# Two bottleneck blocks on one core: the mixed stage's centring in 20 small VectorE operations, its transfers on one queue, and the border's sums and first rows on GpSimd

## The chip, the cores and the metric

The kernel runs on one core of a Trainium2 chip. A core has five engines that run their own instruction streams and wait for each other through semaphores: TensorE (PE in the profile; its weight loads are PEld), VectorE (DVE), ScalarE (ACT), GpSimd (POOL) and SyncE (SP), which here does nothing but issue transfers (DMAs). ACT and GpSimd can issue transfers too. The metric is the device time of one execution in microseconds (us). Before the change it is 1934.73 us, the median of 3 runs (1934.0 to 1935.46).

## The reference

Two residual bottleneck blocks, one after the other, on 64 images of 14 x 14 with 1024 channels, all in float32. The second block has weights of its own. Every batch norm takes its mean and variance from the batch.

```python
def _bn(x, gamma, beta):
    mean = jnp.mean(x, axis=(0, 2, 3), keepdims=True)
    var = jnp.var(x, axis=(0, 2, 3), keepdims=True)
    xn = (x - mean) * jax.lax.rsqrt(var + EPS)
    return gamma.reshape(1, -1, 1, 1) * xn + beta.reshape(1, -1, 1, 1)

def _L0_conv_ref(x, w1, b1, g1, be1, w2, b2, g2, be2, w3, b3, g3, be3, residual_scale):
    out = jax.nn.relu(_bn(_conv(x, w1, b1, 1, 0), g1, be1))     # 1x1, 1024 -> 256
    out = jax.nn.relu(_bn(_conv(out, w2, b2, 1, 1), g2, be2))   # 3x3, 256 -> 256
    out = _bn(_conv(out, w3, b3, 1, 0), g3, be3)                # 1x1, 256 -> 1024
    out = jax.nn.softplus(residual_scale)[0] * out
    out = x + out
    return jax.nn.relu(out)
```

## The kernel before

**Tiles.** The 64 images are 32 tiles of two images, 392 pixels each. Channels lie on the 128 partitions: 1024 channels are 8 slots (`CS`), 256 are 2 slots (`MS`). The output of a block's 3x3 convolution, `y_all`, stays on the chip as a whole: per partition 2 slots of 32 x 392 pixels.

**Stages, by the trace.** The first 1x1 convolution of block 0 runs to about 300 us, its 3x3 convolution to 586, then the *mixed stage* (`mixed`, L1434 to L1650) to about 820, a short *border* to 844, and then `fused`, in which the third convolution of block 0 and the first of block 1 alternate, to about 1280. Block 1's 3x3 convolution and its final stage take the rest.

**Why there is a mixed stage.** The batch norm behind the third convolution needs the mean and variance of the convolution's output. For tiles 16 to 31 (`KEPT` = 16) the stage computes that output, takes its statistics and stores it in DRAM (`z`). For tiles 0 to 15 it computes only the Gram matrix of the convolution's input, from which the statistics follow, and the convolution itself is done later, in `fused`. TensorE alternates between the two.

**The convolution part.** `first()` does tile 16 plainly, with eight outputs, and prepares tile 17 behind the first of them. Then `direct_stream` (L597) runs 60 *units*, four for each of the tiles 17 to 31 (unit = 4 x (tile - 17) + q). A unit is a `Direct`: a 2 x 2 block product done with 7 products of half-size blocks, for which sums of the input's blocks (`ct`, four for each tile) and of the weights are needed. Each unit takes 7 steps, each with one product of this unit or of the one before it: p1 of this unit, p7 of the one before, p5, p2 and p6 of this one, p4 and p3 of the one before. The products land in PSUM banks (`cy`, `cp`, `cx`, `ay`). ACT copies them out (into `kept`, or into the buffers `cu` and `cx`), and DVE adds (L584 and L590) and takes statistics (L595). A bank is free for a later product only when its reader on ACT or DVE is done. `kept` has four slots, one for each q. After a unit's last add its slot goes out to `z` in one transfer on SP's queue (L592; `put`, L1536, for tile 16), and the unit four later writes the same slot again, at its step 2, which has to wait until the transfer has landed.

**The input of a unit.** `prepare(t)` works a tile ahead, on GpSimd: for each of the two slots two operations (`normed_less`, L1510) that scale, shift, clip at 0 and subtract a constant `c` (add `minus_c`), and then four sums of 128 x 196 (`column_sums`, L470 to L473). The loop takes its three steps in units with q = 0 and 1.

**The Gram part.** Tiles 0 to 15 are 6272 pixels, cut into five pieces (`MOVES`: four of 1280 and one of 1152). Each piece goes through this chain:

- *norm* (`norm_piece`): ACT, in 8 parts, one per unit at step 1 (the first 8 in `first()`);
- *centring* (`center`, L1450): `minus_c` is added, one operation for each of the two slots;
- *move* (`move`, L1481): 16 transfers bring `y_all` to `home` with the 32-pixel blocks so arranged that a 32 x 32 transpose on DVE gives pixels on partitions. There are two `home` buffers. Move 0 comes after `first()`, the moves 1 to 4 at the units 9, 17, 25 and 33;
- *transposes* (`turn`, L1244): DVE, 512 columns each, into `zt`;
- *Gram products* (`gram_products`, L159 with `ap<-zt`): TensorE, 32 products at step 2 of the units 9, 12, 15 and so on up to 45. `batches` hands them out: products at step 2, then the transposes of the next batch at step 3 of this unit and of the next.

At units 20, 23, 26 and 29 DVE also combines weights of the next block at step 3 (`summed_a`).

**Order.** Everything in this stage is held in program order on each engine: the order in which the code issues it. So an operation that waits holds up all that stands behind it on its engine, and a transfer on SP's queue stands behind the ones issued before it. `pinned` extends this to helpers that use `run`.

**The border.** When the statistics are there, `residual` finishes tile 0, and `fused` starts: the third convolution of the first kept tiles (`Conv3`, whose block sums are made in `column_sums`, here on DVE), rows of tiles that come back from `z` (`kept_rows`: for odd o GpSimd scales L1798 and adds L1799, for even o DVE does both in one operation L1801), and the first convolution of block 1 (`Conv1`, with copies `au` on ACT). GpSimd also adds for `Conv3` (L530, L535). ACT's relus of finished rows and its copies stand in one order.

**The constant.** `minus_c` is computed once for each block, at the block's start (L2058), into one buffer of a pool under one name: the second block's write has to wait for the last reader of the first block's.

## Time and profile before

| | |
|---|---|
| median of 3 runs | 1934.73 us (1934.0 to 1935.46) |
| the profiled execution | 1934.27 us |
| its span in the trace | 1932.5 us |
| mean granted TensorE clock | 0.994 |
| instructions | 28607 |

The span goes from the first to the last instruction that the profiler recorded; the execution's own time is 1.8 us longer. The timeline view has one row for each instruction, or run of like instructions: start in us, length in us, engine, line of the kernel, operation, output <- input by the program's names, shape, count, and in brackets the idle time of the engine just before it with what ended that. "SPq" is SP's queue of transfers. Matmuls all have L159, and ACT's operations L332, since helpers issue them: they are told apart by what they write and read. The windows view gives the busy time of each engine in a stretch, with the number of instructions in brackets, then the granted TensorE clock (1.00 is full speed), the share of time in which the transfer engines were busy, and the GB/s moved.

### The profile page before, as it was taken

How to read it: one execution, taken by the hardware profiler on the slowest of the kernel's cores; microseconds unless marked ns; L12 is line 12 of the kernel's file. 1: busy time of each engine (PE TensorE's matmuls, PEld its weight loads, DVE VectorE, ACT ScalarE, POOL GpSimd, SP SyncE). 2: the span in 40 equal slices, each digit the busy share in tenths (PEclk: the TensorE clock that was granted, in tenths of full speed). 3: DMA queues.
4: the chain of work that ended last, by engine and by line, in shares of the span. 5: the costliest groups of instructions: out<-in, count | busy, mean ns of one | idle time of the engine just before them, and what ended most of it. 6: DMA issues, size and time to landing. Idle time of an engine off the chain costs nothing. (4 is left out here: it accounts for less than half of the span.)

```text
span 1932.5 us, 28607 instructions
## 1 busy us (share of the span) xinstructions
PE 1890.3 (98%) x9778; PEld 1567.6 (81%) x9778; DVE 1578.1 (82%) x2454; ACT 1089.1 (56%) x2275; POOL 768.1 (40%) x772
## 2 busy tenths in 40 slices
PE   9999999999998889989999999999999999999999
PEld 5555557999996778889999999989999987555555
DVE  5777768999996666777888878789999987888886
ACT  2222214677775454455555555546777782666666
POOL 0111100211206646166777677602112041766665
PEclk9999999999999999999999999999999999999999
DMA  7777634887953445677877789748878557699997
GB/s 290 276 246 267 221 148 158 206 222 201 228 188 121 137 147 167 203 280 279 312 269 287 289 311 263 265 148 208 222 214 216 166 148 278 249 334 342 342 356 280
DMA packets 261986, 458.20 MB, mean 237 GB/s; under 512 B 59152, under 2 KB 228464, under 8 KB 248656
## 3 DMA queue, kind: packets, MB, share of 16 engines
q1 hardware_dynamic: 224608, 374.23, 57.8%
q0 software_dynamic: 31472, 29.47, 7.7%
q10 hardware_dynamic: 5760, 52.67, 6.8%
q8 instruction: 78, 1.28, 0.3%
q14 instruction: 68, 0.56, 0.1%
HBM read 289.44 MB, written 141.03 MB: 223 GB/s over the span
## 5 line engine op out<-in xcount | busy, mean ns | idle before, releaser
L332 ACT ACTIVATE x<-x,shift 128x392 f32<-128x392 f32 x452 | 260.0, 613 | 80.5 <-DVE x L507 31.4
L159 PE MATMUL columns<-v,ub 128*128 128x224 f32 (+1 forms) x1536 | 302.4, 338 | 1.1 <-ACT columns L332 0.8
L159 PEld LDWEIGHTS columns<-v,ub 128*128 128x128 f32 x1536 | 268.8, 188 | 7.0 <-ACT columns L332 1.5
L332 ACT ACTIVATE cu<-cy,scale 128x196 f32<-128x196 f32 (+1 forms) x360 | 175.7, 500 | 167.0 <-PE cy L159 159.9
L159 PE MATMUL ay<-at,ws 128*128 128x196 f32 (+1 forms) x768 | 194.1, 384 | 5.1 <-ACT au L332 3.8
L159 PEld LDWEIGHTS ay<-at,ws 128*128 128x128 f32 x768 | 137.3, 191 | 40.5 <-ACT au L332 4.1
L507 DVE SCALAR_TENSOR_TENSOR x<-cp,scale,x 128x196 f32<-128x196 f32 (+1 forms) x240 | 124.5, 519 | 46.2 <-PE cp L159 44.8
L634 POOL TENSOR_TENSOR x<-x,cu 128x392 f32<-128x392 f32 x120 | 125.8, 1049 | 73.0 <-DVE x L507 71.8
L332 ACT ACTIVATE au<-ay 128x196 f32<-128x196 f32 (+1 forms) x140 | 53.9, 385 | 173.9 <-PE ay L159 159.7
L159 PE MATMUL l<-diffs,ub 128*128 128x224 f32 (+1 forms) x768 | 149.6, 337 | 0.3 <-ACT sd L1894 0.3
L159 PE MATMUL m<-sums,ua 128*128 128x224 f32 (+1 forms) x752 | 146.0, 336 | 0.2 <-DVE sums L750 0.2
L159 PEld LDWEIGHTS l<-diffs,ub 128*128 128x128 f32 x768 | 134.6, 189 | 1.2 <-ACT sd L1894 0.6
L159 PEld LDWEIGHTS m<-sums,ua 128*128 128x128 f32 x752 | 131.5, 189 | 1.3 <-DVE sums L750 0.7
L159 PE MATMUL cx<-y,w 128*128 128x196 f32 (+1 forms) x396 | 126.2, 404 | 0.8 <-ACT cx L332 0.8
L1048 POOL DMA_DIRECT2D y<-f x24 | 32.7, 1683 | 231.8 <-DVE f L968 231.8
L530 POOL TENSOR_TENSOR x<-x,cu 128x196 f32<-128x196 f32 (+1 forms) x120 | 104.5, 871 | 50.9 <-ACT cu L332 22.5
L159 PE MATMUL cy<-y,w 128*128 128x196 f32 (+1 forms) x364 | 115.4, 404 | 1.8 <-POOL y L1510 1.0
L535 POOL TENSOR_TENSOR x<-x,cu 128x392 f32<-128x392 f32 x60 | 79.2, 1320 | 86.1 <-DVE x L507 83.2
L332 ACT ACTIVATE y<-y,shift,scale 128x1568 f32<-128x1568 f32 (+7 forms) x94 | 106.7, 1154 | 6.6 <-DVE shift L1926 6.5
L206 POOL DMA_DIRECT2D u<-y x48 | 26.0, 545 | 212.0 <-ACT y L332 211.3
L159 PE MATMUL cy<-ct,wt 128*128 128x196 f32 x400 | 100.3, 333 | 5.8 <-ACT cu L332 4.7
L1798 POOL TENSOR_SCALAR y<-y,scale 128x392 f32<-128x392 f32 x57 | 94.0, 1649 | 29.4 <-DVE scale L2116 29.4
(298 smaller groups left out, 4551.6 us busy)
## 6 DMA issues: line engine op xcount, KB each, us to landing
ub<-u SPq DMA_DIRECT2D x92, 768.0 KB, 5.2
x<-in_x SPq DMA_DIRECT2D x35, 1568.0 KB, 8.2
mid<-x ACTq DMA_DIRECT2D x32, 1568.0 KB, 8.4
x<-mid SPq DMA_DIRECT2D x32, 1568.0 KB, 8.9
out<-x SPq DMA_DIRECT2D x123, 392.0 KB, 8.1
x<-in_x SPq DMA_DIRECT2D x108, 392.0 KB, 8.1
z<-kept SPq DMA_DIRECT2D x64, 392.0 KB, 3.0
ua<-u SPq DMA_DIRECT2D x92, 256.0 KB, 3.0
```

Of the source, the lines that this page charges most:

```text
L159: tc.keep_in_program_order(nc.tensor.matmul(*args, **kw))
L206: nc.gpsimd.dma_start(out=us[b][i][:, s, o], in_=u)
L332: tc.keep_in_program_order(nc.scalar.activation(*args, **kw))
L507: run(nc.vector.scalar_tensor_tensor(v, bank, self.scale[:, o : o + 1], v, ALU.mult, ALU.add))
L530: run(nc.gpsimd.tensor_add(self.part(1, 1), self.part(1, 1), u3))
L535: run(nc.gpsimd.tensor_add(v, v, self.u12))
L634: nc.gpsimd.tensor_add(v, v, self.u12[:, i * self.n : (i + 1) * self.n])
L1048: nc.gpsimd.dma_start(out=out_rows[3][:, o], in_=fa[:, o, :full], accum_op=ALU.add)
L1798: run(nc.gpsimd.tensor_scalar(z, z, scale[:, o : o + 1], None, ALU.mult))
```

## The change

1. *Centring.* Each piece is centred in four operations (two halves of 640 columns, or 576, for each of the two slots) in place of two, and all of them are on VectorE; before, GpSimd did one slot of the pieces 1 to 4. The loop issues one half at step 3 of a unit as soon as the norm parts that it needs have been issued, as long as a move is still to come: by the order of the instructions that is every even unit from 2 to 32. The four halves of piece 0 come one after another behind `first()`.
2. *Move 0.* All 16 transfers are on SP's queue; before, every second one was on GpSimd's.
3. *Preparation.* The generators of `prepare` are made ahead (`coming`), and `first()` also takes the two `normed_less` steps of tile 18. The loop goes on from there: sums of tile 18, `normed_less` of tile 19, and so on, each at the place where the step before it was.
4. *Transposes.* `batches` yields once more at its start, and the loop starts it at step 3 of unit 8: the first two transposes move there from step 2 of unit 9. The other transposes and all Gram products stay where they were.
5. *Border.* The four block sums of the first `Conv3` in `fused` are made by GpSimd at step 5 of unit 57, into a part of `y_all` that is free by then (`ahead`); DVE made them in the border before. `kept_rows` issues the four GpSimd rows (o = 1, 3, 5, 7) of the first tile that comes back in one go at its start, ahead of GpSimd's adds for `Conv3`; before, they alternated with them.
6. *minus_c.* A tag, and so a buffer, for each block: the second block's operation has no earlier reader to wait for, and stands at the program's start.

The order of the instructions on TensorE and ACT stays as it was; on DVE, GpSimd and SP it differs in the mixed stage and the border, and by the place of L2058.

```diff
@@ -460,13 +460,20 @@
         def after7(self):
             self.result(1, 1, self.p, self.saved("au3"))
 
-    def column_sums(pool, ys, n, twice=(2, 3), eng=nc.vector):
+    def ahead():
+
+        a = (NG - 2) * GPX
+        return [y_all[:, 0, a + i * PX // 2 : a + (i + 1) * PX // 2] for i in range(4)]
+
+    def column_sums(pool, ys, n, twice=(2, 3), eng=nc.vector, to=None, made=False):
 
         sums = []
         for i in range(4):
-            v = pool.tile([P, n], FP, tag=f"ct{i}", name=f"ct{i}", bufs=1 + (i in twice))
+            v = to[i] if to else pool.tile([P, n], FP, tag=f"ct{i}", name=f"ct{i}", bufs=1 + (i in twice))
             sums.append(v.rearrange("p (h l) -> p h l", l=G * W))
         t1, t2, t3, t4 = sums
+        if made:
+            return sums
         run(eng.tensor_sub(t3, ys[1][1], ys[0][1]))
         run(eng.tensor_add(t2, t3, ys[0][0]))
         run(eng.tensor_sub(t1, ys[0][1], ys[0][0]))
@@ -1466,19 +1473,24 @@
             x = homes[k % 2][:, : MS * (e - a)].rearrange("p (s j f) -> p s j f", s=MS, j=4)
             return x, a, (e - a) // 4
 
-        def center(k, engines):
-            a, e = pieces[k]
-            assert normed[k] == 4 * MS
-            for s, eng in enumerate(engines):
-                less(y_all[:, s, a:e], s, eng)
+        centered = collections.Counter()
+
+        def center():
+
+            k = next((k for k in range(len(pieces)) if centered[k] < MS * 2), None)
+            if k is not None and normed[k] >= 2 * centered[k] + 2:
+                s, i = divmod(centered[k], 2)
+                a, e = pieces[k]
+                h = (e - a) // 4 * 2
+                less(y_all[:, s, a + i * h : a + i * h + h if i == 0 else e], s)
+                centered[k] += 1
 
         def move(k):
-            assert k < 2 or k - 2 in turned
+            assert centered[k] == MS * 2 and (k < 2 or k - 2 in turned)
             x, a, run = home(k)
             for i, j in itertools.product(range(4), range(4)):
-                queue = nc.gpsimd if k == 0 and (4 * i + j) % 2 else nc.sync
                 tc.keep_in_program_order(
-                    queue.dma_start(
+                    nc.sync.dma_start(
                         out=x[32 * i : 32 * i + 32, :, j],
                         in_=y_all[32 * j : 32 * j + 32, :, a + i * run : a + i * run + run],
                     )
@@ -1525,7 +1537,7 @@
                 if row:
                     put(t, q)
                 if i == 0:
-                    for _ in itertools.chain(summed_c, prepare(t + 1)):
+                    for _ in itertools.chain(summed_c, prepare(t + 1), itertools.islice(coming[t + 2], MS)):
                         pass
                 if 2 < i < 7:
                     next(norms)
@@ -1560,6 +1572,7 @@
             queue, total = chunks(), NGRAM // P
             bounds = [*range(0, total, BATCH), total]
             ready = [list(itertools.islice(queue, BATCH))]
+            yield
             for a, e in zip(bounds, bounds[1:]):
                 for i, (v, _) in zip(range(a, e), ready.pop()):
                     gram_products(upper, lower, v, i == 0, i == total - 1, True)
@@ -1570,17 +1583,19 @@
                     yield
 
         norms = itertools.chain.from_iterable(norm_piece(k) for k in range(len(pieces)))
+        coming = {t: prepare(t) for t in range(KEPT + 1, T)}
         first()
         both = psum.tile(512, "ap")
         upper, lower = both[:, : 3 * Q + 1], both[:, 3 * Q + 1 : 5 * Q + 3]
         zts, by, gs = gram_tiles(pool, NGRAM, 3)
-        center(0, (nc.vector, nc.vector))
+        for _ in range(2 * MS):
+            center()
         move(0)
-        coming, tail, grams = iter(()), None, iter(())
+        tail, grams = None, iter(())
         moves = {9: 1, 17: 2, 25: 3, 33: 4}
         at = list(range(9, 48, 3))
         at_first, _ = beds((None, None))
-        made = []
+        made, done = [], []
 
         def make(*tags):
             for tag in tags:
@@ -1603,20 +1618,20 @@
         pinned.append(True)
         for unit, step in direct_stream(units(), between, finish):
             t, q = KEPT + 1 + unit // 4, unit % 4
-            if step == 0 and q == 0 and t + 1 < T:
-                coming = prepare(t + 1)
             if step == 1 and unit > 0:
                 next(norms, None)
-            if step == 2 and unit == at[0]:
+            if step == 3 and unit == at[0] - 1:
                 grams = batches()
+                next(grams)
             if step == 2 and unit in at or step == 3 and (unit in at or unit - 1 in at):
                 next(grams, None)
             if step == 3:
-                if q < 2:
-                    next(coming, None)
-                if unit + 1 in moves:
-                    center(moves[unit + 1], (nc.vector, nc.gpsimd))
+                if q < 2 and t + 1 < T:
+                    next(coming[t + 1], None)
+                if len(moves) > len(done):
+                    center()
                 if unit in moves:
+                    done.append(unit)
                     move(moves[unit])
                 if unit in (20, 23, 26, 29):
                     next(summed_a)
@@ -1631,8 +1646,10 @@
                         nc.gpsimd.memset(to[:, :, 0], NGRAM / 2)
                         run(nc.vector.tensor_copy(to[:, :, 1], mv3[:, :, 0]))
                         run(nc.vector.tensor_scalar(to[:, :, 2], mv3[:, :, 1], NGRAM / 2, None, ALU.mult))
-            if step == 5 and q == 1:
-                next(coming, None)
+            if step == 5 and q == 1 and t + 1 < T:
+                next(coming[t + 1], None)
+            if step == 5 and unit == 57:
+                column_sums(pool, blocks(positions()[2]), n, eng=nc.gpsimd, to=ahead())
             if unit == 59 and step in (3, 5):
                 aggregated(step // 4)
             if step == 6 and unit > at[-1] + 1 and (tail is None or unit < 57):
@@ -1777,7 +1794,7 @@
             for p in range(2, T, 2):
                 t = places[p]
                 ys = [[two(t, s)[:, i * H // 2 : (i + 1) * H // 2] for i in range(2)] for s in range(MS)]
-                sums = column_sums(pool, ys, n)
+                sums = column_sums(pool, ys, n, **(dict(to=ahead(), made=True) if p == 2 else {}))
                 for q in range(CS // 2):
                     yield Conv3(psum, pool, xs[p], q, n, ys, sums, w3, aff, mids[t] if q == CS // 2 - 1 else None, one)
 
@@ -1787,16 +1804,26 @@
 
         def kept_rows():
 
+            def row(r, p, o):
+                v, z = xs[p][:, o, :], at[r] if r < len(at) else whole[0][:, o]
+                if len(z.shape) > 2:
+                    v = v.rearrange("p (h l) -> p h l", h=H)
+                return v, z
+
+            def by_pool(v, z, o):
+                run(nc.gpsimd.tensor_scalar(z, z, scale[:, o : o + 1], None, ALU.mult))
+                run(nc.gpsimd.tensor_add(v, v, z))
+
+            for o in range(1, CS, 2):
+                by_pool(*row(o, 1, o), o)
             for r, (p, o) in enumerate(itertools.product(range(1, T, 2), range(CS))):
                 while r == len(at) and later:
                     later.pop(0)()
                     yield
-                v, z = xs[p][:, o, :], at[r] if r < len(at) else whole[0][:, o]
-                if len(z.shape) > 2:
-                    v = v.rearrange("p (h l) -> p h l", h=H)
+                v, z = row(r, p, o)
                 if o % 2:
-                    run(nc.gpsimd.tensor_scalar(z, z, scale[:, o : o + 1], None, ALU.mult))
-                    run(nc.gpsimd.tensor_add(v, v, z))
+                    if p > 1:
+                        by_pool(v, z, o)
                 else:
                     run(nc.vector.scalar_tensor_tensor(v, z, scale[:, o : o + 1], v, ALU.mult, ALU.add))
                 for q in behind[r]:
@@ -2054,7 +2081,7 @@
 
     for b in range(2):
         pb = par[b]
-        minus_c = keep.tile([P, MS], FP, tag="minus_c", name="minus_c")
+        minus_c = keep.tile([P, MS], FP, tag=f"minus_c{b}", name="minus_c")
         nc.vector.tensor_scalar(minus_c, pb[:, BE2 : BE2 + MS], 0.0, -1.0, ALU.max, ALU.mult)
         stats2 = keep.tile([P, MS, 1 + PARTS, nc.vector.BN_STATS_DIM], FP, tag="stats2", name=f"stats2_{b}")
         with tc.tile_pool(name=f"conv2_{b}", bufs=1, reuse_waits="tile") as pool, ExitStack() as scope:
```

## The prediction

> **What bounds the kernel now.** The page comes first: span, busy shares, then the busy time by stage, whose columns are window, length, busy time of PE, PEld, DVE, ACT and POOL, granted TensorE clock, DMA share, GB/s.
>
> ```profile
> span 1932.5 us, 28607 instructions
> PE 1890.3 (98%) x9778; PEld 1567.6 (81%) x9778; DVE 1578.1 (82%) x2454; ACT 1089.1 (56%) x2275; POOL 768.1 (40%) x772
> ```
>
> ```profile
> 0.00:586.00 586.00, 581.45 (x2472) 443.74 (x2472) 486.63 (x626) 271.46 (x537) 73.13 (x114) 1.00 0.70 219
> 586.00:844.00 258.00, 230.16 (x1398) 198.17 (x1399) 171.25 (x362) 133.47 (x378) 138.93 (x143) 0.95 0.53 175
> 844.00:1932.50 1088.50, 1078.68 (x5910) 925.68 (x5908) 920.17 (x1468) 684.18 (x1361) 556.05 (x516) 1.00 0.79 262
> ```
>
> TensorE bounds everything. Of its 42 us of idle time, 28 lie in the 258 us that the change touches (mixed stage and border), and only there is the clock below 1.00. So I read that stretch of PE's timeline for rows with an idle time (in brackets, with what ended it):
>
> ```profile
> 612.20 1.02 PE L159 MATMUL cp<-ct,wt 128*128 128x196 f32 x2 [3.33 <-POOL ct L472]
> ...
> 630.14 0.60 PE L159 MATMUL ay<-ct,wt 128*128 128x196 f32 x2 [2.81 <-DVE kept L590]
> 632.09 4.00 PE L159 MATMUL ap<-zt 128*64 128x193 f32 x32 [1.35 <-DVE zt L1244]
> 663.01 1.02 PE L159 MATMUL ay<-ct,wt 128*128 128x196 f32 x2 [2.81 <-DVE kept L590]
> 678.08 0.93 PE L159 MATMUL ay<-ct,wt 128*128 128x196 f32 x4 [1.55 <-ACT cu L332]
> 709.63 0.60 PE L159 MATMUL cy<-ct,wt 128*128 128x196 f32 x2 [4.07 <-ACT cu L332]
> 726.34 0.60 PE L159 MATMUL ay<-ct,wt 128*128 128x196 f32 x2 [2.40 <-DVE kept L590]
> 784.18 0.60 PE L159 MATMUL cp<-ct,wt 128*128 128x196 f32 x2 [1.27 <-DVE kept L590]
> ...
> 840.17 1.67 PE L159 MATMUL ay<-at,ws 128*128 128x196 f32 x4 [3.77 <-ACT au L332]
> ```
>
> 630, 663 and 726 are units 8, 16 and 32, each one before a move: DVE's add L590, which frees a PSUM bank, stood behind the centring.
>
> ```profile
> 625.62 3.52 POOL L1450 TENSOR_SCALAR y<-y,minus_c 128x1280 f32<-128x1280 f32 x1 [3.39 <-ACT y L332]
> 625.88 3.94 DVE L1450 TENSOR_SCALAR y<-y,minus_c 128x1280 f32<-128x1280 f32 x1
> ```
>
> 678 and 709 (units 20, 28) come from the moves: SP needs 10.6 us for 16 issues, the `z` stores stand behind them, and ACT waits for a store before it writes a slot of `kept` again.
>
> ```profile
> 663.63 10.59 SPq L1481 DMA_DIRECT2D home<-y  x16
> 677.25 0.33 ACT L332 ACTIVATE kept<-cp 128x196 f32<-128x196 f32 x1 [2.19 <-DMA z<-kept]
> ```
>
> From move to restart of PE: 678.08 - 663.63 = 14.45. A second price follows the longer stalls:
>
> ```profile
> 615.00:618.30 3.30, 3.30 (x12) 3.30 (x11) 1.77 (x4) 1.54 (x4) 3.04 (x5) 0.50 0.24 93
> ...
> 662.60:666.10 3.50, 3.08 (x9) 3.09 (x10) 1.67 (x5) 1.07 (x4) 3.24 (x4) 0.51 0.49 161
> 676.30:679.70 3.40, 1.84 (x16) 1.34 (x16) 1.92 (x6) 2.13 (x7) 3.30 (x4) 1.00 0.82 298
> 710.40:713.90 3.50, 3.50 (x12) 3.50 (x12) 1.98 (x5) 1.50 (x5) 0.00 (x0) 0.51 0.31 117
> 727.50:731.00 3.50, 3.50 (x29) 2.71 (x24) 0.73 (x2) 0.00 (x0) 3.34 (x6) 0.51 0.68 206
> ```
>
> After stalls of 2.4 us and more the clock is at half for one window of 3.4 us, which costs 1.7 us of work if PE is busy in all of it; after 1.55 us it is not. The Trainium skill ("TensorE: Matmul & The Clock Gate", Part 1: What's actually happening) lets the clock drop only after at least one whole idle window of about 3.4 us. The trace differs: the half clock at 662.6 follows a gap of 2.81. By that rule the clock terms of the shorter gaps in the sum below (unit 9's 1.6, unit 20's 1.1, unit 36's 1.2) would be zero, and the sum -6.3 in place of -8.0.
>
> **The change part by part.** Signs: minus is time saved; units are counted along the trace.
>
> *Start.* Move 0 goes from two queues to SP alone.
>
> ```profile
> 594.89 0.59 POOL L473 TENSOR_TENSOR ct<-y,ct 128x196 f32<-128x196 f32 x1
> 601.08 4.38 POOL L1481 DMA_DIRECT2D home<-y  x8 [5.60 <-DVE kept L584]
> 605.49 0.68 POOL L1510 TENSOR_SCALAR y<-y,scale,shift 128x392 f32<-128x392 f32 x1
> 608.64 1.59 POOL L1510 TENSOR_SCALAR y<-y,minus_c 128x392 f32<-128x392 f32 x1
> ```
>
> ```profile
> 585.77 0.42 DVE L1450 TENSOR_SCALAR y<-y,minus_c 128x392 f32<-128x392 f32 x1
> 598.71 1.66 DVE L1450 TENSOR_SCALAR y<-y,minus_c 128x1280 f32<-128x1280 f32 x2
> ```
>
> ```profile
> 616.28 0.86 PE L159 MATMUL cy<-ct,wt 128*128 128x196 f32 x2
> ```
>
> GpSimd's 8 issues and their 4.38 go, and its four norm operations (605.49 to 610.23, so 4.74) now follow the sums of tile 17, from 595.48 to 600.2. The 3.33 for late sums at 612.20 therefore goes. What is late next is `kept`: the stores of tile 17 stand behind 16 issues in place of 8. DVE's four halves, beside GpSimd until 600.2, end near 601.5, so PE restarts at 601.5 + 14.45 = 615.95, against 616.28: -0.3. The idle time, now in one piece of some 4 us, puts a whole half-clock window behind it as at 710.40 (1.7), where before only 1.0 was left of one (616.28 to 618.3 at 0.50): +0.7. **Sum +0.4**, bounds -0.7 (move at 600.4, as the halves alone, 4 x 0.55, would allow) and +2.4 (move at 603.5, halves held up as at 625.88).
>
> *Centring.* A half of 640 columns takes 0.55 by the two DVE rows (0.42 for 392, 0.83 for 1280). The other bound is a half locked behind a GpSimd operation: at 625 the two engines' operations, 0.83 alone on DVE, took 3.5 and 3.9 together, and GpSimd's commonest one takes 1.59. So 0.55 to 2.15 for each (0.55 and one whole 1.59 of waiting); I take the lower end, and single waits where the order of GpSimd's work puts an operation beside a half. DVE's room in a unit ahead of L590 I estimate at one transpose, 0.7: units with one transpose, as the one at 639.27 below, show no idle PE. A half alone in its unit is covered by that and costs nothing (with the cover gone, 0.55); a half beside a transpose or a combination of weights is not. 3.3 of GpSimd's own time for each centring goes too, which nobody waits for.
>
> ```profile
> 639.27 0.69 DVE L1244 STREAM_TRANSPOSE zt<-home 128x512 f32<-128x512 f32 x1
> 643.45 2.41 PE L159 MATMUL ap<-zt 128*64 128x193 f32 x32
> ```
>
> Unit 8: two transposes and a half, 2 x 0.69 + 0.55, less 0.7 of room, and 0.2 of lock: 1.4 in place of 2.81: **-1.4**. Unit 9: the wait of 1.35 for transposes goes, and the gram products run at full clock, as at 643.45 (2.41 in place of 4.00), since 1.4 at unit 8 is below the stalls that halve it: **-2.95**. Unit 16: -2.81 and +0.7 for a lock: **-2.1**. Unit 32: **-2.2** (0.2 for a lock stays). New: unit 14, a half behind a 1.59 operation, **+0.7**; units 10 and 22, transpose and half together (0.69 + 0.55 - 0.7), with 24: **+0.7**. Without any lock waits (0.2 + 0.7 + 0.7 + 0.2 and 0.3 of the last term) the sum is 2.1 less; with one at every half it is a rival below.
>
> The Trainium skill ("SBUF — State Buffer", Who interferes with whom) speaks against this part: VectorE and GpSimd share an exclusive lock on a port, and the loser waits in full. The rows at 625 agree. By that rule more small operations mean more chances to wait.
>
> *The moves.* Their 16 issues stay, so PE's restart 14.45 after a move's start stays too. Unit 20: PE arrives earlier, by the half clock that unit 16 no longer causes, and waits longer, 3.1 in place of 1.55: no gain, and a half clock behind it, which I take at two chances in three: **+1.1**. Unit 28: its chain (move at 694, wait 4.07) keeps its length: **0** (-1.2 if a transpose waits less). Units 12 and 36 hid this wait behind gram products:
>
> ```profile
> 644.40 0.33 ACT L332 ACTIVATE kept<-cp 128x196 f32<-128x196 f32 x1 [0.69 <-DMA z<-kept]
> 738.27 2.41 PE L159 MATMUL ap<-zt 128*64 128x193 f32 x32
> 740.29 0.34 ACT L332 ACTIVATE kept<-cp 128x196 f32<-128x196 f32 x1 [2.33 <-DMA z<-kept]
> ```
>
> PE needs the bank 4.0 after its gram products begin (2.4 and five products of 0.33), and has it 0.83 after ACT's row: spare 2.3 at 643.45, 1.2 at 738.27. Unit 12 is reached 2.5 earlier (2.95 less 0.45 at unit 10): **+0.2**. Unit 36 is reached 1.7 earlier, the window at 727.50 being gone, and 0.5 of that turns into a wait: **-1.2**.
>
> *minus_c.* DVE waited for the name, and L590 behind it:
>
> ```profile
> 783.70 0.17 DVE L2058 TENSOR_SCALAR minus_c<-par 128x2 f32<-128x2 f32 x1 [3.16 <-POOL y L1510]
> ```
>
> A name for each block frees it: **-1.27**.
>
> *Border.*
>
> ```profile
> 827.90 0.57 PE L159 MATMUL cy<-ct,wt 128*128 128x196 f32 x2 [1.03 <-DVE ct L471]
> ...
> 835.37 2.78 POOL L1798 TENSOR_SCALAR y<-y,scale 128x392 f32<-128x392 f32 x1
> 838.24 1.01 POOL L1799 TENSOR_TENSOR x<-x,y 128x392 f32<-128x392 f32 x1
> ```
>
> The 1.03 for DVE's sums goes (GpSimd makes them at unit 57, four of 0.59, beside nothing that waits for it). But the end of this stretch is set by `au` at 840.17. ACT gives it out in order behind relus, which wait for GpSimd: first for rows, later for the adds L530 and L535, now queued behind four rows. The rows begin as before; at 2.4 each (less than 3.79, the contended pair shown) the adds end early enough for -2.6, at 3.4 they end +2.5 late. I take **0**.
>
> Sum: 0.4 - 1.4 - 2.95 - 2.1 - 2.2 + 0.7 + 0.7 + 1.1 + 0.2 - 1.2 - 1.27 = **-8.0**. The profiled execution took 1934.27 (1.8 outside its span), 0.46 under the median 1934.73: 1926.3 and 1926.7. Forecast **1926.5**. Its own range is 1921 to 1931: upward the start (+2) and the border (+2.5), downward the lock waits (-2.1), unit 28 and the border in part.
>
> **Rivals.**
>
> *The lock decides, slower (0.11).* If halves take 2.15, those which no wait for stores swallows later add to the path: 1.6 more each at units 8, 10 and 22, and 2.15 - 0.7 = 1.45 each at units 14, 16 and 32, together 9.15, less the 1.8 already counted: +7.3. The same lock costs the border +2.5 and the start +1.7: -8.0 becomes +3.5, 1938. It decides from a mean half of 1.5 us, where its first part is some 4 and the gain is half gone. For it: 625.88. Against it: GpSimd is busy in half of this stretch only (138.93 of 258).
>
> *SP's queue paces the stage, no change (0.15).* What DVE gives back at units 8, 16 and 32 is waited for again behind the 16 issues: the gains of units 9 and 36 (4.2) and the start (+1.7) go so, and -8.0 becomes -2.2: 1932.5. For it: the 4.07 at 709.63, which the change leaves. Against it: units 8, 9, 16 and 32 lie ahead of or at a move's start, and a chain that starts earlier also ends earlier.
>
> *More than forecast (0.17).* No lock waits (-2.1), no half clock at unit 20 (-1.1), 28 gains (-1.2), border -2.6: 1919.5.
>
> The forecast has 0.57. A change under 0.2% (3.9 us) can't be told from none here. Faster by more: 0.57 and 0.17, less the forecast's upper end, 0.72; same 0.17; slower 0.11. The range leaves the slow rival out and reaches from the best case to just over the no-change one: **1919 to 1933**.
>
> **What would show it.** DVE's centring rows should be 0.5 to 0.8 us on the mean; over 1.5 the lock rival holds. PE's waits at units 16 and 32 should be gone or under 1; unit 9's gram products should take 2.4. SP should show one block of 16 issues near 601, and ACT's first wait for `z` near 614. Unit 20's wait should grow to 3 us, with a half clock behind it. No DVE row of L2058 should stand in the stage. `au` should land within 2.6 us of its old place in the border. The forecast is wrong if stores behind moves wait at units 12 and 36 too, or if anything outside 586 to 844 moves by more than 1 us.

## The result and the profile after

The changed kernel takes 1925.05 us (median of 5 runs, 1919.95 to 1926.35) against 1934.91 us before (median of 5): ratio 0.9943, 95% interval [0.9927, 0.9958]. The profiled execution took 1926.02 us, 8.25 less than the one of before.

The page's head, then the busy time by stage (columns as in the prediction). The border ends 8 us earlier now, so the middle stretch is cut at 836:

```profile
span 1924.2 us, 28592 instructions
...
PE 1889.5 (98%) x9778; PEld 1569.0 (82%) x9778; DVE 1573.1 (82%) x2464; ACT 1087.6 (57%) x2275; POOL 748.5 (39%) x764
```

```profile
0.00:586.00 586.00, 581.51 (x2471) 444.60 (x2472) 485.46 (x624) 270.75 (x537) 73.04 (x114) 1.00 0.70 219
586.00:836.00 250.00, 229.61 (x1405) 196.61 (x1404) 167.05 (x374) 134.17 (x382) 121.67 (x135) 0.96 0.54 181
836.00:1924.20 1088.20, 1078.43 (x5905) 927.83 (x5903) 920.58 (x1468) 682.65 (x1358) 553.74 (x516) 1.00 0.79 262
```

The whole gain is in the middle stretch: 250 us for 258, with PE's busy time the same (229.6 and 230.2) and its idle time 20.4 in place of 27.8. The last stretch keeps its length within 0.3 us.

PE's timeline of the changed kernel, at the places that answer to the rows of the prediction (a row without brackets has no wait ahead of it):

```profile
587.41 2.90 PE L159 MATMUL cy<-y,w 128*128 128x392 f32 x8 [0.73 <-DVE y L1457]
...
616.17 1.02 PE L159 MATMUL cy<-ct,wt 128*128 128x196 f32 x2 [4.62 <-ACT cu L332]
629.55 0.60 PE L159 MATMUL ay<-ct,wt 128*128 128x196 f32 x2 [0.78 <-DVE kept L597]
630.08 2.41 PE L159 MATMUL ap<-zt 128*64 128x193 f32 x32
645.34 0.60 PE L159 MATMUL cy<-ct,wt 128*128 128x196 f32 x2 [0.97 <-ACT cu L332]
658.25 0.60 PE L159 MATMUL ay<-ct,wt 128*128 128x196 f32 x2
672.99 1.67 PE L159 MATMUL ay<-ct,wt 128*128 128x196 f32 x4 [2.72 <-ACT cu L332]
706.83 1.02 PE L159 MATMUL cy<-ct,wt 128*128 128x196 f32 x2 [3.29 <-ACT cu L332]
721.41 0.77 PE L159 MATMUL ap<-zt 128*64 128x193 f32 x8
737.33 0.60 PE L159 MATMUL cy<-ct,wt 128*128 128x196 f32 x2 [1.88 <-ACT cu L332]
777.75 0.49 PE L159 MATMUL cp<-ct,wt 128*128 128x196 f32 x2
831.55 0.93 PE L159 MATMUL ay<-at,ws 128*128 128x196 f32 x4 [2.07 <-ACT au L332]
```

The waits for DVE at units 16 and 32, for transposes at unit 9, for GpSimd near 612 and for `minus_c` are gone. What is left ends with ACT: five waits (616, 645, 673, 706, 737) are stores of `z` behind a move, 13.5 us together. Two rows of the kernel before serve as further marks, the stage's first product and the product behind unit 32:

```profile
586.24 2.90 PE L159 MATMUL cy<-y,w 128*128 128x392 f32 x8 [0.74 <-DVE y L1450]
```

```profile
726.86 0.38 PE L159 MATMUL ap<-zt 128*64 128x193 f32 x2
```

The products of TensorE stand in the same order in both kernels, so the same product can be found in both. The next table sets the start in the changed kernel against the start before; the fourth column is what the stretch since the last mark gained or lost; the last is what the prediction's terms give for that stretch.

| mark (before, after) | later by | in this stretch | predicted |
|---|---|---|---|
| stage begins (586.24, 587.41) | +1.17 | +1.17 | 0 |
| restart at unit 4 (616.28, 616.17) | -0.11 | -1.28 | -0.3 |
| unit 8 (630.14, 629.55) | -0.59 | -0.48 | +0.7 - 1.4 = -0.7 |
| unit 9's Gram products (632.09, 630.08) | -2.01 | -1.42 | -1.35 |
| unit 16 (663.01, 658.25) | -4.76 | -2.75 | -1.6 + 0.45 + 0.2 + 0.7 - 2.1 = -2.35 |
| unit 20 (678.08, 672.99) | -5.09 | -0.33 | 0 |
| unit 28 (709.63, 706.83) | -2.80 | +2.29 | +1.1 + 0.25 = +1.35 |
| behind unit 32 (726.86, 721.41) | -5.45 | -2.65 | -2.2 |
| minus_c (784.18, 777.75) | -6.43 | -0.98 | -1.2 - 1.27 = -2.47 |
| border (840.17, 831.55) | -8.62 | -2.19 | 0 |
| end of span (1932.5, 1924.2) | -8.3 | +0.32 | 0 |

The second price, the clock, is in the windows view of the changed kernel:

```profile
669.10:672.50 3.40, 1.17 (x8) 0.86 (x6) 2.69 (x5) 0.35 (x2) 3.30 (x5) 1.00 0.82 273
672.50:675.90 3.40, 2.91 (x14) 2.29 (x16) 1.45 (x3) 1.77 (x6) 3.30 (x3) 0.50 0.69 253
675.90:679.30 3.40, 3.40 (x27) 2.59 (x24) 0.00 (x0) 0.00 (x0) 0.19 (x1) 0.50 0.00 0
733.90:737.40 3.50, 1.62 (x11) 1.32 (x9) 1.25 (x3) 0.91 (x5) 2.36 (x3) 1.00 0.72 260
737.40:740.80 3.40, 3.40 (x20) 3.26 (x21) 2.59 (x7) 2.10 (x8) 2.72 (x3) 1.00 0.33 122
```

Behind the wait at 673 PE ran two windows at half clock; behind the 1.88 us at 737 none.

### The profile page after: what moved, and what is told of

Its sections match the earlier page's. It is cut to its first block, busy times and chain, and to the rows that moved or that the text cites. A ratio compares the mean times of both kernels' runs of the same rounds, so it can differ in the third digit from the quotient of the medians.

```text
span 1924.2 us, 28592 instructions
## 1 busy us (share of the span) xinstructions
PE 1889.5 (98%) x9778; PEld 1569.0 (82%) x9778; DVE 1573.1 (82%) x2464; ACT 1087.6 (57%) x2275; POOL 748.5 (39%) x764
## 3 DMA queue, kind: packets, MB, share of 16 engines
q8 instruction: 78, 1.28, 0.3%
## 5 line engine op out<-in xcount | busy, mean ns | idle before, releaser
L332 ACT ACTIVATE au<-ay 128x196 f32<-128x196 f32 (+1 forms) x140 | 53.8, 384 | 173.1 <-PE ay L159 158.9
L537 POOL TENSOR_TENSOR x<-x,cu 128x196 f32<-128x196 f32 (+1 forms) x120 | 104.8, 873 | 48.6 <-ACT cu L332 27.8
L159 PE MATMUL cy<-ct,wt 128*128 128x196 f32 x384 | 96.4, 333 | 10.9 <-ACT cu L332 10.8
L936 ACT ACTIVATE columns<-m 128x448 f32<-128x448 f32 (+1 forms) x144 | 70.9, 492 | 58.9 <-PE m L159 54.0
```

The lines of the kernel that those rows point to most:

```text
L159: tc.keep_in_program_order(nc.tensor.matmul(*args, **kw))
L332: tc.keep_in_program_order(nc.scalar.activation(*args, **kw))
L537: run(nc.gpsimd.tensor_add(self.part(1, 1), self.part(1, 1), u3))
L936: copy(v, m, AF.Copy)
```

## The experiments

All of them start from the changed kernel, and each is timed beside runs of the kernel before. Times of the changed kernel spread by 6 us from one execution to the next, so besides the ratio I use a quieter number: the sum of all waits over 0.12 us in PE's timeline from 584 to 850 (28.3 us before, 20.2 in the changed kernel's first profile).

| kernel | ratio to before, 95% interval | PE's waits, us | half-clock windows, 590 to 850 |
|---|---|---|---|
| before | 1 | 28.3 | 7 |
| changed | 0.9943 [0.9927, 0.9958] | 20.2 | 6 |
| changed, once more | 0.9939 [0.9924, 0.9954] | 20.4 | 2 |
| whole slots, DVE and GpSimd | 0.9987 [0.9978, 0.9997] | 25.0 | 7 |
| whole slots, DVE alone | 0.9961 [0.9946, 0.9976] | 23.8 | 5 |
| transposes back | 0.9941 [0.9925, 0.9956] | 19.7 | 5 |
| move 0 on two queues | 0.9917 [0.9898, 0.9937] | 17.1 | 2 |
| tile 18 not ahead | 0.9940 [0.9920, 0.9960] | 20.0 | 3 |
| minus_c shared | 0.9940 [0.9926, 0.9955] | 22.1 | 2 |
| border back | 0.9958 [0.9943, 0.9973] | 20.6 | 4 |
| rows back | 0.9951 [0.9936, 0.9966] | 22.1 | 2 |
| moves in parts | 0.9889 [0.9872, 0.9905] | 13.8 | 2 |
| moves in parts, earlier | 0.9864 [0.9848, 0.9881] | 9.9 | 0 |
| moves in parts, earlier and larger | 0.9849 [0.9834, 0.9864] | 7.6 | 1 |

**The changed kernel once more.** No edit.

> The changed kernel once more, beside the other three. Both theories: ratio to the kernel before 0.9925 to 0.996. The theory of the clock (half-clock windows lie on a grid that runs free of the kernel, so that the same stall costs one window, two or none) expects times that spread by 3 to 6 us, and in this profile another count of half-clock windows than the 6 of the changed kernel's profile, with stalls of the same length (4.6, 1.0, 2.7, 3.3, 1.9 us for stores behind moves). The rival, that the spread comes from the transfers, expects the same windows and stalls of other lengths.

1920.87 us (1920.46 to 1926.62). Its waits are the first profile's within 0.42 us each (4.60, 1.23, 2.70, 3.71 and 1.49 for stores), its half-clock windows are 2 in place of 6, and its span is 1918.7 in place of 1924.2. The wait before 671.30 is as long as the one before 672.99, but it lies across two windows:

```profile
671.30 0.93 PE L159 MATMUL ay<-ct,wt 128*128 128x196 f32 x4 [2.70 <-ACT cu L332]
```

```profile
669.70:673.10 3.40, 1.80 (x18) 1.48 (x19) 1.62 (x4) 2.12 (x7) 3.20 (x5) 1.00 0.81 298
673.10:676.50 3.40, 3.40 (x34) 3.11 (x30) 0.65 (x2) 1.00 (x3) 1.34 (x1) 1.00 0.22 77
```

The same stall costs no clock here and 3.2 us there (two windows at half speed). The theory of the clock holds for these two. Of the other executions only the time and the mean granted clock are on record, and the two go together: 0.995 at 1926.02, 1926.35 and 1926.62 us, 0.997 at 1920.46 to 1921.19, 0.998 at 1919.95. So the spread between executions is mostly the place of the windows. The intervals reach some 0.0015, or 3 us, to each side, so kernels that differ by less can't be told apart by their ratios, and the waits decide.

**The centring: parts or engine?** Two kernels centre pieces 1 to 4 in whole slots again at the unit before each move; the first gives one slot to GpSimd as before, the second has both on DVE. `center_whole` does what `center` did in the kernel before.

```diff
-                if len(moves) > len(done):
-                    center()
+                if unit + 1 in moves:
+                    center_whole(moves[unit + 1], (nc.vector, nc.gpsimd))
```

> The changed kernel with pieces 1 to 4 centred as before: one whole slot on DVE and the other on GpSimd at the unit before each move (piece 0 stays in halves on DVE). Theory that the small parts are what took the waits at units 8, 16 and 32 away: they come back with 2.4 to 3 us each, the waits for z at units 12, 20 and 36 shrink by 1 to 2 us in return, and the kernel is 3 to 7 us slower than the changed one. Rival, that what helped was moving the transposes ahead and the end of GpSimd's transfers: the waits at 16 and 32 come back, but z's waits shrink by as much, and the time is within 1.5 us of the changed kernel.

> The changed kernel with pieces 1 to 4 centred in whole slots of 1280 columns at the unit before each move, but both on DVE (piece 0 in halves as in the changed kernel). It tells the size of the operations from the engine. If the lock between the two engines made the old waits (two operations of 0.83 took 3.5 and 3.9 us side by side), DVE alone takes 2 x 0.83 = 1.7 to 2.2 us, which is 1.0 to 1.5 over the room of 0.7: PE waits 1 to 1.5 at units 16 and 32 and 2 to 2.4 at unit 8 (with two transposes), and the time is 0 to 3 us above the changed kernel, ratio 0.994 to 0.996. If it was the size, the waits are 2.4 to 2.9 as with GpSimd, and the ratio is 0.997 to 0.999.

With GpSimd, all three waits are back, and with them most of the time (0.9987, 1931.74 us); two of the three, and the pair of operations at unit 16:

```profile
629.81 1.02 PE L159 MATMUL ay<-ct,wt 128*128 128x196 f32 x2 [2.81 <-DVE kept L597]
...
662.89 0.67 PE L159 MATMUL ay<-ct,wt 128*128 128x196 f32 x2 [2.86 <-DVE kept L597]
```

```profile
658.37 3.52 POOL L1457 TENSOR_SCALAR y<-y,minus_c 128x1280 f32<-128x1280 f32 x1 [8.64 <-ACT y L332]
```

```profile
658.95 3.62 DVE L1457 TENSOR_SCALAR y<-y,minus_c 128x1280 f32<-128x1280 f32 x1
```

On DVE alone, both slots together take less than one slot beside GpSimd, and PE's wait is half as long:

```profile
658.74 2.20 DVE L1457 TENSOR_SCALAR y<-y,minus_c 128x1280 f32<-128x1280 f32 x2
```

```profile
661.26 0.60 PE L159 MATMUL ay<-ct,wt 128*128 128x196 f32 x2 [1.46 <-DVE kept L597]
```

So of the 2.86 us at unit 16 about half was GpSimd as a partner, and the rest the size of the block. The waits came as expected (2.81, 2.86 and 2.40 with GpSimd; 1.93, 1.46 and 1.02 with DVE alone), the times a little above: with DVE alone 0.9961, with GpSimd 9 us above the changed kernel by the ratios (0.9987 and 0.9939, timed together), where 3 to 7 were expected. Its sum of waits is 4.6 us higher, and it had 7 half-clock windows where the other profile had 2.

**Transposes back.**

```diff
-            if step == 3 and unit == at[0] - 1:
+            if step == 2 and unit == at[0]:
```

> The changed kernel with the first two transposes at step 2 of unit 9 again. The prediction priced them with the clock, as 1.35 + 1.6 us. Theory now: PE waits 1.35 at unit 9 again, its 0.8 at unit 8 goes, and the 1.0 to 1.2 at unit 12 shrinks by what is left: within 0.7 us of the changed kernel in the sum of PE's waits, and no half clock at unit 9, since no stall of 2 us stands ahead of it. Rival, that the prediction's size holds for this part alone: about 3 us slower, with a half-clock window at unit 9.

```profile
630.63 2.42 PE L159 MATMUL ap<-zt 128*64 128x193 f32 x32 [1.35 <-DVE zt L1251]
```

The wait of 1.35 is back, the 0.8 at unit 8 and the 1.0 to 1.2 at unit 12 are gone, and the products run at full clock (2.42). The sum of waits is no higher (19.7 against 20.2 and 20.4), but the wait at unit 12 is not the transposes' doing (see "Units 12 and 36" below). So moving the transposes ahead is worth some 0.6 us by itself, 1.35 less 0.78. The half clock that unit 9 lost came from the 2.81 us of centring ahead of it: with that back, in the kernel with whole slots on both engines, the clock is at half there again (629.1 to 636.0).

**The start.** Of the preparation only tile 18's steps stand elsewhere in the changed kernel, the two of `normed_less` in `first()` and the sums at unit 0 in place of unit 1; those of tile 19 and later come at the units where they were (not each one place earlier, as the list of the change says). Two kernels: every second transfer of move 0 back on GpSimd's queue, and `first()` without the two steps of tile 18.

```diff
+                queue = nc.gpsimd if k == 0 and (4 * i + j) % 2 else nc.sync
                 tc.keep_in_program_order(
-                    nc.sync.dma_start(
+                    queue.dma_start(
...
-                    for _ in itertools.chain(summed_c, prepare(t + 1), itertools.islice(coming[t + 2], MS)):
+                    for _ in itertools.chain(summed_c, prepare(t + 1)):
```

> The changed kernel with every second transfer of move 0 on GpSimd's queue again. Theory that the norm of tile 18, done earlier, and not the transfers taken from GpSimd, ended the waits for GpSimd near 612, and that the 16 issues on SP only put the wait of 4.6 us for z at unit 4 in their place: SP's part ends 5 us earlier, the sums of tile 18 are still in time, and the wait of 4.6 us shrinks to under 1: 2 to 6 us faster than the changed kernel, ratio 0.9905 to 0.993. Rival, that GpSimd's own issues would make the sums of tile 18 late again: a wait for GpSimd of 1 to 4 us near 612, and the time within 2 us of the changed kernel or above it.

> The changed kernel without the two steps of tile 18 in first(). GpSimd's four operations of tile 18 then stand ahead of the sums of tile 17 in its order, so PE should wait some 3 to 5 us for those sums near 598. Theory that move 0's chain alone sets the restart at unit 4 (14.3 us after the move's start, which hangs on ACT's norm and DVE and not on PE): the wait of 4.6 us at unit 4 shrinks by as much, the restart stays within 1 us of 14.3 after the move's start, and the sum of waits up to there stays within 1.5 us of the changed kernel's 6.6. Rival, that the chain hangs on PE's work too: the restart comes 3 to 5 us later and the waits add up to 9 to 11.

With two queues:

```profile
601.18 5.49 SPq L1494 DMA_DIRECT2D home<-y  x8
```

```profile
611.79 0.60 PE L159 MATMUL cy<-ct,wt 128*128 128x196 f32 x2 [1.30 <-ACT cu L332]
```

No wait for GpSimd, and the 4.62 us at unit 4 are 1.30 (under 1 was expected): 1917.58 us, ratio 0.9917 where the changed kernel had 0.9939 and 0.9943. The intervals overlap, but the wait at unit 4 was 4.60 to 4.62 in both profiles of the changed kernel: taking the transfers from GpSimd lost 3.3 us there. The expectation for the other kernel was wrong in its first half: without the early steps GpSimd did tile 18's four operations even earlier (585.39 to 590.1), while it would have waited for ACT, ahead of the sums of tile 17, and PE did not wait for them. The second half held: move at 601.55, restart 14.25 later.

```profile
601.55 10.39 SPq L1493 DMA_DIRECT2D home<-y  x16
```

```profile
615.80 1.02 PE L159 MATMUL cy<-ct,wt 128*128 128x196 f32 x2 [4.93 <-ACT cu L332]
```

In both kernels tile 18's operations no longer stand behind GpSimd's issues, and the old wait near 612 is gone in both. The first shows that doing them earlier is enough, with the issues left on GpSimd. Whether taking the issues away would have been enough too is not shown, since in the second kernel the operations came earlier as well.

**minus_c.**

```diff
-        minus_c = keep.tile([P, MS], FP, tag=f"minus_c{b}", name="minus_c")
+        minus_c = keep.tile([P, MS], FP, tag="minus_c", name="minus_c")
```

> The changed kernel with one name for minus_c in both blocks again. Theory: DVE's operation for the second block waits for GpSimd near 777 and PE for 1.3 us behind it: 1.0 to 1.6 us slower than the changed kernel, in the profile one more wait of PE of that length and no other. Rival, that the wait was cover for a later one: the same time, with another wait gone.

```profile
774.56 0.17 DVE L2085 TENSOR_SCALAR minus_c<-par 128x2 f32<-128x2 f32 x1 [3.45 <-POOL y L1522]
```

```profile
775.04 0.60 PE L159 MATMUL cp<-ct,wt 128*128 128x196 f32 x2 [1.56 <-DVE kept L597]
```

One wait more, 1.56 us, and no other of the changed kernel's waits gone. The timing can't show it (0.9940 against 0.9939 and 0.9943).

**The border.** As before in both parts, and in the rows alone.

```diff
-            for o in range(1, CS, 2):
-                by_pool(*row(o, 1, o), o)
...
-                    if p > 1:
-                        by_pool(v, z, o)
+                    by_pool(v, z, o)
```

> The changed kernel with the border as before: DVE makes the first Conv3's sums in the border, and GpSimd's rows alternate with its adds. The prediction gave the border 0. The traces give it -2.2 us between the stage's end and the first au. If that is the change's own work, this kernel is 2 to 3 us slower than the changed one, and PE waits 3 to 4 us for au and 1 us for DVE's sums again. If it is only where the half-clock window fell, the wait for au stays near 2.1 us and the time is within 1 us.

> The changed kernel with GpSimd's rows of the first tile alternating with its adds again, but the first Conv3's sums still made at unit 57. Theory that the rows alone made the border's gain (the sums' wait of 1.03 for DVE came back as 0.93 for ACT): PE waits 3.5 to 3.8 for au in place of 2.07 and the rest of the border is as in the changed kernel: 1.5 to 2 us slower in the sum of waits, without a difference in the first three waits of the border. Rival, that both parts are needed, since the sums free DVE for the even rows: the wait for au is near 2.1 or 3 or more than 4.

In both, PE waits 3.77 us for `au` in place of 2.07. The rows alone:

```profile
818.17 0.60 PE L159 MATMUL cy<-y,wt 128*128 128x196 f32 x2 [0.93 <-ACT cu L332]
...
829.16 0.93 PE L159 MATMUL ay<-at,ws 128*128 128x196 f32 x4 [3.77 <-ACT au L332]
```

The border's waits are 5.21 us with both undone, 5.11 with the rows undone and 3.40 in the changed kernel. The rows are worth 1.7 us and the sums on GpSimd 0.1: the 1.03 for DVE's sums came back as 0.93 for ACT. So the border's gain is the change's own work, in the rows alone.

**Moves in parts.** The five waits left in the changed kernel all have a move's 16 issues ahead of a store. Three kernels hand these issues out over units: first 4 per unit at step 3; then with moves 1 to 4 begun a unit earlier and move 0 in parts of 3; then with parts of 6 for moves 3 and 4. The cut shows the third.

```diff
-            for i, j in itertools.product(range(4), range(4)):
+
+            def one_block(i, j):
                 tc.keep_in_program_order(
                     nc.sync.dma_start(
...
+            to_move.extend(partial(one_block, i, j) for i, j in itertools.product(range(4), range(4)))
...
-        moves = {9: 1, 17: 2, 25: 3, 33: 4}
+        moves = {8: 1, 16: 2, 24: 3, 32: 4}
...
+                for _ in range(min(3 if unit < 8 else 4 if unit < 24 else 6, len(to_move))):
+                    to_move.pop(0)()
```

> The changed kernel with the 16 issues of each move handed out 4 per unit over four units, in place of all at once. Theory that SP's queue sets the five remaining waits for z: they go (13.5 us in the changed kernel's profile), and with them the half-clock windows behind three of them (about 6 us): 15 to 19 us faster than the changed kernel, ratio to the kernel before 0.985 to 0.987. Rival, that the landing of transfers and not their place in the queue sets the waits, or that pieces now come home too late for the transposes: waits of 2 to 4 us stay, at the same units or at DVE's transposes, and the gain is under 5 us, ratio above 0.991.

> The kernel that hands a move's issues out over units, mended where its trace still waits: moves 1 to 4 begin one unit earlier (8, 16, 24, 32), and move 0 goes out in parts of 3 rather than 4. Theory that the waits left there are transposes that wait for the last parts of a move (0.6, 0.7, 0.7, 0.6 and 2.3 us of PE) and stores behind the parts of move 0 (0.4 and 1.8): they go, 4 to 7 us faster than that kernel, ratio to the kernel before 0.985 to 0.987. Rival, that the queue is as full as before and the wait only moves on to the stores: no more than 2 us faster, ratio 0.988 to 0.9895, with waits of ACT for z in the units 11 to 14.

> The second version that hands a move's issues out over units, with 6 in place of 4 per unit for the moves 3 and 4, where DVE's transposes waited 1.0 and 4.0 us for a piece to come home and PE 1.4 and 1.0 behind them. Theory that there the parts came too slowly: both waits of PE go or halve, 1 to 2 us faster in the sum of waits, ratio 0.985 to 0.987. Rival, that these waits are a transpose and a half of the centring in one unit, and no transfer: the waits stay.

The first took 1912.69 us, 8 less than the changed kernel beside it, rather than the 15 to 19 expected: the stores no longer waited, except twice behind move 0, but transposes waited for the last parts of a move. The theory of the queue was right and my schedule late. The second took 1907.2 us, 5.5 less, as expected: no wait for a store is left, but two for the transposes of moves 3 and 4 are. The third took 1905.4 us: PE's waits at 691 and 720 in the second's trace, 1.39 and 1.00 us, are 0.19 and none; 0.8 at unit 8 and 0.7 at unit 20 stay, where DVE has more work in one unit than it has room for. In its trace the stores pass between the parts of the move, and PE works through the whole stage at full clock:

```profile
604.92 0.57 SPq L599 DMA_DIRECT2D z<-kept  x1
605.53 1.90 SPq L1495 DMA_DIRECT2D home<-y  x3
607.54 0.57 SPq L599 DMA_DIRECT2D z<-kept  x1
```

```profile
600.00:740.00 140.00, 137.75 (x998) 123.57 (x999) 99.77 (x221) 85.76 (x252) 82.14 (x96) 1.00 0.53 171
```

## Why the prediction was right, and where its steps were off

The forecast was 1926.5 us, the measured median 1925.05, the sum -8.0 against -8.25 between the profiled executions. The mechanism was right in the main: the waits that the change was to remove are gone, and the gain lies in the stretch where it was placed. That the numbers agree so closely is in part luck. The profiled execution had six half-clock windows; the ratios of both sets of runs, 0.9943 and 0.9939, mean -11.0 and -11.8 us. And the terms agree less well than the sum: the stretches of the table add up to -9.8 from the stage's beginning to the border's end, and 1.17 us that the execution lost ahead of the stage (the changed kernel's second profile begins the stage at 586.30, so this is no work of the change) hide the difference.

*Right in kind, and near in size.* The centring's waits at units 8, 16 and 32, the transposes' wait and half clock at unit 9 (1.35 us of waiting and 4.00 - 2.41 of products, 2.94 for 2.95), `minus_c` (1.56 us when it is put back), and the price of move 0: restart 14.3 us after its start, for 14.45. The start itself, 601.88, is 600.7 without the 1.17 us, 0.8 earlier than the 601.5 of the prediction, and so the first stretch gained 1.28 and not 0.3. The wait at unit 20 grew to 2.72 us, for 3.1; the one at unit 28 shrank from 4.07 to 3.29, where I had left it as it was. In the stretch to unit 8 two errors cancel: two half-clock windows behind unit 4 (614.5 to 621.3) cost 1.6 us more than before, for 0.7, and the wait at unit 8 shrank by 2.0, for 1.4.

*Room on DVE.* I put DVE's room ahead of L590 at 0.7 us, from units with one transpose and no wait. That is only a lower bound. Unit 16 now has a transpose and a half in it, 1.4 us, and PE did not wait:

```profile
656.57 0.69 DVE L1251 STREAM_TRANSPOSE zt<-home 128x512 f32<-128x512 f32 x1
657.19 0.73 DVE L1457 TENSOR_SCALAR y<-y,minus_c 128x640 f32<-128x640 f32 x1
```

Unit 8 (two transposes and a half of 0.70, 2.1 us) waited 0.78, so the room is some 1.3. The terms of units 10, 14 and 16 and of 22 with 24 (0.45 + 0.7 + 0.7 + 0.25) should have been near zero: at units 10, 16 and 22 a product starts 0.2 us late without a wait that the view shows (at 637.13 behind 636.58, where the usual step is 0.33). By the prediction's own formula, 0.69 + 0.55 - 0.7, units 10 and 22 would have cost 1.1 together, where it put 0.7.

*The lock.* The centring's line, with the shortest, median and longest of its operations in ns (the 392-column one is tile 16's):

```profile
L1457 DVE TENSOR_SCALAR y<-y,minus_c x21: 419/540/882, 586.9 to 719.6; 128x640 f32<-128x640 f32 x16, 128x576 f32<-128x576 f32 x4, 128x392 f32<-128x392 f32 x1
```

No half took over 0.88 us, and the slow rival, which needed 1.5, fell with that. It did not fall because the halves met no long GpSimd operation. Five of the 20 halves ran beside one of 1.59 to 1.84 us and took 0.48 to 0.54, as long as the five that ran beside nothing. One of them, with the GpSimd operation that began before it and ended after it:

```profile
604.99 1.59 POOL L1522 TENSOR_SCALAR y<-y,minus_c 128x392 f32<-128x392 f32 x1
```

```profile
605.64 0.54 DVE L1457 TENSOR_SCALAR y<-y,minus_c 128x640 f32<-128x640 f32 x1
```

Nine ran beside GpSimd's block sums (L477 to L480) and took 0.70 to 0.88, and one more took 0.81. So a half behind an operation of 1.59 us did not wait for it, and the terms that I put down for such a wait had no ground. The Trainium skill ("SBUF — State Buffer", Who interferes with whom) lets the loser of the shared port wait in full. The two large operations side by side again took 3.5 and 3.6 us and the same work on DVE alone 2.20 for both, which agrees. For the halves the trace does not agree, as far as its spans for GpSimd go: none took more than 0.34 us above the 0.54 of an undisturbed one.

*The clock.* I expected one half-clock window behind unit 20 at two chances in three; there were two, 3.2 us, and in the next execution none. The Trainium skill ("TensorE: Matmul & The Clock Gate", Part 1: What's actually happening) has the window run free of the kernel, and the two profiles agree with that. With its condition for the drop, a whole idle window, they do not agree: 2.2 idle us in the window from 669.1 were enough. Nor was one window the rule: the kernel before already had two in a row near its stall at 612 (611.5 to 618.3), and I had read only the second.

*Units 12 and 36.* The prediction named two signs against itself: that stores behind moves wait at units 12 and 36 too, and that something outside 586 to 844 moves by more than 1 us. Both came, the second only as the 1.17 us above. At unit 12 I gave +0.2, and PE waited 0.97. At unit 36 I gave -1.2: 1.7 earlier, 0.5 of it waited. It was reached 1.5 earlier and waited 1.88. The move's 10.3 us were as before, but the store behind it released ACT 4.6 us after its issue:

```profile
731.86 6.19 SPq L599 DMA_DIRECT2D z<-kept  x4
```

```profile
736.49 0.33 ACT L332 ACTIVATE kept<-cp 128x196 f32<-128x196 f32 x1 [5.61 <-DMA z<-kept]
```

In the kernel before it was 2.9 us, from this row to ACT's at 740.29:

```profile
737.36 5.83 SPq L592 DMA_DIRECT2D z<-kept  x4
```

The traces show what came in between. The list of DMA queues from 732.5 to 734.5 in the changed kernel has, beside the queue of the transfers, one packet of 16 KB:

```profile
q8 instruction: 1, 0.02, 4.7%
```

It began at 732.90 and took 1.51 us, while the store was under way (731.86 to 736.41). In the kernel before it came at 741.12, when the store had landed (740.21). The eleven profiles of kernels that issue their moves in one go have 55 stores that stand first behind a move. Of these, 36 landed 2.82 to 2.86 us after their issue, and none of them had such a packet in it. The other 19 took 3.79 to 4.96: 16 with a packet that had begun by 1.2 us after the issue, one with a packet 2.9 us after it, and two, behind move 0 on two queues, without one. At unit 12 the store took 3.80 in the changed kernel, and 2.83 with the transposes back, where PE did not wait. With 2.85 in both places I estimate no wait at unit 12 (0.97 - 0.95) and 0.2 at unit 36 (1.88 - 1.71): so 2.7 of the 13.5 us of waits for stores belong to the packet, and the queue rival was not right there. (Its price was also mis-summed: the gains that it takes back at units 8, 16 and 32 are 5.7 us, and it counted the 4.2 of units 9 and 36.) No run moved the packet on purpose, and what sets its place is open.

*Border.* I took 0 between two bounds, -2.6 with rows of 2.4 us and +2.5 with rows of 3.4. It was -2.2, and the first bound's row length decided. Taking the middle of two bounds was the error: the term was -2 (53.8 us from `minus_c` to `au`, 55.8 with the border as before). GpSimd's four rows in one go, first and last:

```profile
816.34 1.28 POOL L1814 TENSOR_SCALAR y<-y,scale 128x392 f32<-128x392 f32 x1 [29.38 <-DVE scale L2143]
...
825.06 1.04 POOL L1815 TENSOR_TENSOR x<-x,y 128x392 f32<-128x392 f32 x1
826.06 0.60 POOL L537 TENSOR_TENSOR x<-x,cu 128x196 f32<-128x196 f32 x1
```

Four rows in 9.7 us, 2.4 each. The 2.78 us of the long row belonged to its place later in the border, which the change vacates. With the rows put back it is there again:

```profile
824.35 2.79 POOL L1814 TENSOR_SCALAR y<-y,scale 128x392 f32<-128x392 f32 x1
```

I should have priced a row by where it goes and not by where it stood.

*What the prediction didn't ask.* Part 2 of the change lost some 3.2 us of waits by itself (17.1 without it, 20.2 and 20.4 with it). The prediction counted GpSimd's 4.38 us of issues as a gain and the stores behind 16 issues as the next thing late, but not that GpSimd's issues, with tile 18's operations ahead of them, would have cost nothing.

## What to carry to other kernels

A block of transfers on one queue is a wait for whatever stands behind it: 16 issues of 0.65 us held five stores back, with 13.5 us of waits behind them (an estimated 2.7 of it by a packet of another queue). Handed out in parts between the stores, with the moves begun a unit earlier, they left no wait for a store in the stage and took another 0.9% off, where the change itself took 0.6%. Price a piece of work by the rows of the place that it goes to, and find an engine's room by how much work made a wait, not by how much did not. Where stalls trip the clock, compare the sum of waits and not one execution's time.

## What the runs showed of the hardware

The half clock has a sharp condition. I laid PE's waits between 590 and 850 us of 13 profiled executions (the fourteenth has no half window there) on the grid of 3.41-us windows that the granted clock shows. After a window at full clock with 1.99 us or more of waiting the next was always at half, after 1.81 or less never. Between these lie eight windows with 1.84 to 1.94: two were followed by a half window and six were not. A half window with 0.34 or less of waiting was followed by full clock, every one with 0.46 or more by another half (as 672.50 above). So a stall of 2.7 us costs nothing (the changed kernel once more), one window (transposes back, tile 18 not ahead) or two (the changed kernel's first profile) by where it falls on the grid, and that is most of the 6 us by which executions of this kernel differ.

A 16-KB packet of the queue "q8 instruction" that falls into a store goes with a landing 0.9 to 1.7 us later: 3.79 to 4.56 us after the issue in 16 cases, 2.82 to 2.86 in 36 without one.
